# Two expert layers on one core: the shared expert's matrix sums through DRAM, and the sums of x in three steps

## The chip, the cores and the metric

The kernel runs on one core of a Trainium2 chip. The metric is device time in microseconds of one execution; the lower the better. The time before is the median of three runs. Durations of single instructions come from one profiled execution of the same kernel.

The engines go by short names: PE (TensorE, matrix products; PEld is its loading of weights), DVE (VectorE), ACT (ScalarE), POOL (GpSimd), SP (SyncE, which here only issues DMAs). Each takes its instructions strictly in the order of the program.

## The reference

The input x has 16 batches of 256 rows by 256 columns in float32, and cond_8 has 16 rows of 8 logits. Two layers of experts follow, each added to its input:

```
# layer 0: one expert per batch, by the largest logit
expert = argmax(cond_8)
up   = x @ W_up[expert].T   + b_up[expert]
gate = x @ W_gate[expert].T + b_gate[expert]
x = x + (silu(up) * gate) @ W_down[expert].T + b_down[expert]
# layer 1: two experts per batch, weighted, and one shared expert
mlp(x, g, u, d) = (gelu(x @ g) * (x @ u)) @ d
w, sel = top_k(softmax(cond_8), 2);  w = w / sum(w)
x = x + sum_k w_k * mlp(x, skill[sel_k]) + mlp(x, shared)
```

Layer 0's hidden width is 512, layer 1's is 1024. The shared expert of layer 1 has the same three matrices for all 16 batches.

## The kernel before

**Pairs and seven products.** Two batches that use the same expert are worked on as a pair. A pair's matrix product is cut into blocks of two by two, and instead of eight block products the kernel makes seven, with sums of blocks on both sides (Winograd's form of Strassen's method). `STEPS` lists the seven: each has a PSUM bank (X, Y or Q), a block or sum of the weights (A11, A12, A22, and sums S1, S2, nS3, nS4) and a block or sum of the activations (B11, B21, B22, T2, nT1, nT3, nT4). Which batches form pairs is decided from the logits while the kernel runs.

A pair's up phase is cut into quarters: two for layer 0 (`kp` 2) and four for layer 1 (`kp` 4), each with its own 512 KB of gate and up weights. A quarter is the seven products of `up`, of which the seventh (`up(j, 6)`, of the Q bank) is put two steps into the next quarter. In between ACT copies three partial results from PSUM (`copy`, line 504) and DVE makes four blocks of the result (`combine`, line 508): C11, then C12 of the quarter before, C22, C21. The seventh product adds to the Q bank that C22 of its quarter has read. Then `act` applies the activation function: for layer 1 ACT's gelu (line 552) and a product by DVE (line 553), for layer 0 ACT's silu (559) and DVE's line 560. The down phase (`down`) is again seven products, interleaved with the next units' quarters; its late results are DVE's lines 606 and 610.

**Sums.** Three kinds of sums feed the seven products:

- `sums_q` (per quarter) and `sums_d` (per pair) make the four sums of the weight blocks through `sums_a` (lines 468 to 471) on POOL: four instructions of 128x256 elements for a quarter and four of 128x256 (layer 0) or 128x512 (layer 1) for the down weights.
- `sums_x` (per pair) makes the sums of the activations through `sums_b` (lines 461 to 463) on DVE: one instruction of 128x512 and two of 128x256, in the tile `xt` (layer 1) or `bt` with `dz` (layer 0).
- `act_sums` (per quarter) does the same with `sums_b` on the activation's result, a full quarter after it.

**Order.** The order of work is written out when the program is built. `Line` has a clock that each of a quarter's six first products moves by 2 (`UP`), so a quarter is 12. `later(after, f)` puts an action into a list; `flush` emits the due actions, the earliest first and in order of entry among equals. In a quarter that starts at 0, the earlier quarter's seventh product and C12 come at 4, its activation at 6, and its `act_sums` at 12. A pair's down products come at 18 and then every 3 (layer 0), 6 (layer 1) or 4 (three of the shared pairs) after its last quarter.

`ahead(i)`, at the start of quarter i, loads the weights of quarter i+5 (`load_q`, on SP), makes the sums of quarter i+3 (`sums_q`), loads x for a pair that starts at i+3, and, if a pair starts at i+1, calls `sums_x` for it: all three sums are emitted there, before quarter i's own products. The down weights' sums come in the third quarter of a layer-1 pair, and at the end of a layer-0 pair.

**Buffers.** `RINGS` holds the SBUF rings: 6 buffers of quarter weights (`q`), 5 of their sums (`s`), 2 of the down sums (`ds`), 2 of layer 1's x with its sums (`xt`), 7 of activations (`bt`). PSUM has two banks each of X, Y and Q and one each of A and B for the down products; down products of step Y take a bank from the same two as the up products, in turn.

**Units and branches.** With this data the order is: two single batches of layer 0; two pairs of layer 0; a branch on how many further pairs there are (`arms(0)`); then two pairs of layer 0, and the shared pairs 0 to 4 with three more layer-0 pairs after the first three of them; then twelve pairs of sparse experts; a second branch (`arms(1)`); shared pair 5, single batches, three more sparse pairs, and shared pairs 6 and 7. [...] `follow` then sets the list of quarters for the arm and loads the weights of the first quarter that wasn't yet loaded; with `behind=True` three tiny writes to the buffer by DVE, POOL and ACT come first (lines 390 to 392), so that this load, and all that follows it on SP, waits until those engines are in the arm.

Of the kernel before, what the change touches and what calls it, by code (L numbers as in the profile page):

```python
# [8 lines left out]
F32 = mybir.dt.float32  # L9
I32 = mybir.dt.int32  # L10
AF = mybir.ActivationFunctionType
ALU = mybir.AluOpType
# [5 lines left out]
P = 128  # L18
KD = D // P
KPS = (H0 // P // 2, H1 // P // 2)  # L20
# [9 lines left out]
QW = 2 * 4 * P  # L30
# [21 lines left out]
C11, C21, C12, C22 = range(4)  # L52
# [7 lines left out]
def kernel(  # L60
# [10 lines left out]
    nc = tc.nc  # L71
# [5 lines left out]
    dram = ctx.enter_context(tc.tile_pool(name="dram", bufs=1, space=bass.MemoryType.DRAM))  # L77
    ps = ctx.enter_context(tc.tile_pool(name="ps", bufs=1, space=bass.MemoryType.PSUM))

    x1d = dram.tile([B, P, KD, S], F32, name="x1d")  # L80

# [365 lines left out]
    class Pair(Unit):  # L447
# [1 line left out]
        first, step = 18, None  # L449


        def sums_x(self):
            self.x = {n: self.xt[:, i, :] for n, i in B_AT.items()}
            if not self.layer:
                self.x["T2"] = take("dz", S, of=(self, "T2"))
            self.sums_b(self.xt, self.x["T2"])

        @staticmethod
        def sums_b(t, t2):
            tt = nc.vector.tensor_tensor  # L460
            tt(t[:, 4:6, :], t[:, 0:3:2, :], t[:, 2:4, :], ALU.subtract)  # L461
            tt(t2, t[:, C22, :], t[:, 4, :], ALU.add)  # L462
            tt(t[:, 6, :], t[:, C21, :], t2, ALU.subtract)

        @staticmethod
        def sums_a(a, s):
# [5 lines left out]

        def sums_q(self, j):
            s = take("s", QB, of=(self, j))
            s = s[:, :QW].rearrange("p (m k h) -> p m k h", m=2, k=4)
            q = self.q[j]
            self.sums_a(lambda n: q[:, :, A_AT[n], :], lambda n: s[:, :, S_AT[n], :])
            self.s[j] = s
            if not self.layer:
                b = take("bq", 4)  # L480
                nc.gpsimd.tensor_copy(b, self.bq[j])
                self.bq[j] = b

        def sums_d(self):
            s = take("ds", 4, KPS[1], P)
            s = s[:, :, : self.kp]
            d = self.d
            self.sums_a(lambda n: d[:, A_AT[n]], lambda n: s[:, S_AT[n]])
            self.ds = s

        def load_z(self):

# [69 lines left out]

        def act_sums(self, j):
            t = self.acts[j]
            self.sums_b(t, t[:, 2, :])

        def down(self, k):

# [202 lines left out]
    units = [l0_pairs[: NP1 - 2], [*pairs, *shared[NF : NPR - NB]]]  # L771
    tails = [l0_pairs[NP1 - 2 :], shared[-NB : 1 - NB]]
# [7 lines left out]
    def in_order(units):  # L780

        order = []
        for u in units:
            for j in range(u.kp):
                order.append((u, j))
                for p in among[u][j] if u.width == 2 else ():
                    one = p.func.__self__ if isinstance(p, partial) else p.__self__
                    if isinstance(p, partial):
                        order.append((one, p.args[1]))
                    elif p == one.ups:  # L790
                        order += [(one, i) for i in range(one.kp)]
        return order

    quarters = [(u, j) for u in (l0_first, l0_one) for j in range(u.kp)]
    quarters += in_order(units[0] + tails[0])
    Q_AHEAD, S_AHEAD = 5, 3

    class Line:
# [24 lines left out]
        def ahead(self, i):  # L823

            at = dict(enumerate(quarters))
            if i + Q_AHEAD in at:
                u, j = at[i + Q_AHEAD]
                u.load_q(j)
            if i + S_AHEAD in at:
                u, j = at[i + S_AHEAD]  # L830
                if u.width == 2:
                    when_free("s", lambda u=u, j=j: u.sums_q(j))
                if j == 0:
                    if u.width == 2 and not u.layer:
                        when_free("bt", u.load_x)
                    else:
                        if u.layer:
                            self.send(0)
                        u.load_x()
            if i + 1 in at:  # L840
                u, j = at[i + 1]
                if u.width == 2 and j == 0:
                    u.sums_x()
            if i < 0:
                return
            u, j = at[i]
# [55 lines left out]
    line = Line()  # L902
# [52 lines left out]
            quarters[:] = order  # L955
            yield k

    def follow(common, units):

        quarters[common - 4 :] = in_order(units)  # L960
        u, j = quarters[common]
        u.load_q(j, behind=True)

    run(units[0])
    for k in arms(0):
        common = len(quarters)

        mid = [*tails[0]]
        for i, u in enumerate(shared[:NF]):
            mid.append(u)  # L970
            if i < k:
                mid.append(l0_more[i])
                u.step = 4
        places = [a for u in mid for a in among[u]]
        for a in places:
            a.clear()
        pieces = [p for u in l0_ones[2 * k :] for p in (u.ups, u.downs)]
        for a, p in zip(places[3:], pieces):
            a.append(p)
        follow(common, [*mid, *units[1], *tails[1]])  # L980
        run([*mid, *units[1]])
        while line.routed < len(steps):
            line.route()
        for k in arms(1):
            common = len(quarters)
            left = ones[2 * k :]
            rest = [*tails[1], *left[:-1], *more_pairs[:k], *shared[1 - NB :]]
            turns["xs"], turns["d"] = [0, 1], [*turns["d"], 2]
            for u in rest:
                among[u] = [[] for _ in range(u.kp)]  # L990
            if left:

                host = rest[len(left)]
                for j in range(host.kp):
                    among[host][j].append(partial(left[-1].piece, line, j, among=True))
                left[-1].po_bank, left[0].po_bank = "A", "B"
                shared[-NB].first = 24
            follow(common, rest)
            run(rest)
            line.flush(1 << 30)  # L1000
            line.send()
# [58 lines left out]
```

## Time and profile before

| | us |
|---|---|
| median of 3 runs | 1076.67 |
| lowest and highest | 1074.55 and 1078.24 |
| the profiled execution | 1075.29 |
| its span, from first to last instruction | 1073.6 |

The granted TensorE clock is 0.994 over the span. DMA moved 132.35 MB, of which queue q1 (SP's) had 118.88 MB, at a mean of 123 GB/s.

How to read the views that follow: a row of busy times by stage gives the stretch, its length, then for PE, PEld, DVE, ACT and POOL the busy time and the number of instructions, then the granted clock, DMA's busy share and its rate in GB/s. A row of waits names who waited, for what, the total in us, how often, and the longest. A row of the timeline gives the start and length in us, the engine, the line of the kernel, the operation, the tiles (written<-read), their shapes and the number of instructions merged; in brackets stands how long the engine was idle before and what ended that. A matrix product of the program shows as two records, so `x4` on PE is two products of 128x128 weights with 256 columns.

### The profile page before, as it was taken

The numbers are of one execution on the slowest core, as the hardware profiler recorded it, in microseconds if no ns is written. First come the engines' busy times: TensorE is split into PE (matmuls) and PEld (weight loads), VectorE is DVE, ScalarE is ACT, GpSimd is POOL, SyncE is SP. The second block draws the span as 40 slices with busy tenths as digits, with TensorE's granted clock in tenths as the row PEclk, the third lists the DMA queues.
The fourth block names the chain that finished last, engine by engine and source line by source line (L and its number), as shares of the span: only waits on it lengthen the run. The fifth ranks groups of instructions, "written<-read, shape, count | busy, mean of one in ns | idle before, by whom it ended". The sixth has DMA issues, their size and how long they took to land.

```text
span 1073.6 us, 14292 instructions
## 1 busy us (share of the span) xinstructions
PE 1045.7 (97%) x4750; PEld 902.5 (84%) x4750; DVE 805.2 (75%) x1222; ACT 353.5 (33%) x556; POOL 582.8 (54%) x642
## 2 busy tenths in 40 slices
PE   9989999899999999999999999999999999999997
PEld 6777878787878888888888888888888888888886
DVE  7879988888798777777787777777876336787774
ACT  2323333333423333333333333333333123333331
POOL 2837644464476646664675476557623245675520
PEclk9999999999999999999999999999999999999999
DMA  7625443435352542454355335533534545344212
GB/s 249 206 91 167 159 136 109 147 118 135 121 157 80 137 130 89 115 137 117 83 135 138 92 92 136 137 104 89 139 93 132 170 128 157 89 137 129 71 37 43
DMA packets 53203, 132.35 MB, mean 123 GB/s; under 512 B 4850, under 2 KB 24434, under 8 KB 49906
## 3 DMA queue, kind: packets, MB, share of 16 engines
q1 hardware_dynamic: 40562, 118.88, 33.8%
q0 software_dynamic: 12256, 12.06, 8.9%
q8 instruction: 43, 0.70, 0.3%
q14 instruction: 54, 0.44, 0.1%
q10 hardware_dynamic: 288, 0.26, 0.1%
HBM read 110.21 MB, written 20.97 MB: 122 GB/s over the span
## 4 chain that ended last, share of the span: by engine, by line
PE 78%; DVE 15%; issue 4%; ACT 2%; POOL 1%; DMA 0%; SPq 0%; DVEq 0%; ACTq 0%; POOLq 0%
PE X L523 20%; PE Q L523 14%; PE Y L523 13%; PE A L577 11%; PE B L577 8%; PE Y L577 7%; DVE c L508 5%; DVE bt L461 2%; PE X L670 2%; PE Q L670 1%; DVE bt L553 1%; ACT c L552 1%; DVE bt L462 1%; PE A L700 1%; DVE bt L560 1%
## 5 line engine op out<-in xcount | busy, mean ns | idle before, releaser
L504 ACT ACTIVATE cp<-X 128x512 f32<-128x512 f32 x318 | 188.7, 595 | 522.7 <-PE X L523 522.3
L523 PE MATMUL Q<-xt,s 128*128 128x256 f32 x736 | 190.9, 382 | 11.1 <-DVE c L508 11.1
L523 PE MATMUL Y<-xt,q 128*128 128x256 f32 x736 | 190.4, 381 | 3.0 <-DVE ys L610 1.8
L553 DVE TENSOR_TENSOR bt<-c 128x1024 f32<-128x1024 f32 x92 | 129.0, 1402 | 85.1 <-ACT c L552 85.0
L523 PE MATMUL X<-xt,s 128*128 128x256 f32 x736 | 189.3, 380 | 0.0
L523 PEld LDWEIGHTS Q<-xt,s 128*128 128x128 f32 x736 | 139.5, 191 | 33.2 <-issue 13.4
L508 DVE TENSOR_TENSOR c<-cp,Q 128x512 f32<-128x512 f32 x212 | 143.9, 679 | 30.6 <-ACT cp L504 27.7
L468 POOL TENSOR_TENSOR s<-q 128x256 f32<-128x256 f32 x106 | 98.4, 928 | 119.4 <-DMA q<-wq_dram 60.1
L523 PEld LDWEIGHTS Y<-xt,q 128*128 128x128 f32 x736 | 138.4, 190 | 26.7 <-DVE c L508 4.7
L523 PEld LDWEIGHTS X<-xt,s 128*128 128x128 f32 x736 | 139.3, 190 | 20.8 <-issue 2.1
L471 POOL TENSOR_TENSOR s<-s,q 128x256 f32<-128x256 f32 x106 | 83.5, 788 | 131.5 <-PE Q L523 131.5
L508 DVE TENSOR_TENSOR c<-cp,Y 128x512 f32<-128x512 f32 x212 | 143.8, 678 | 10.0 <-PE Y L523 9.3
L440 POOL DMA_DIRECT2D out_dram<-ys x46 | 49.6, 1079 | 154.1 <-DVE c L508 62.3
L552 ACT ACTIVATE c<-c 128x1024 f32<-128x1024 f32 x92 | 96.8, 1052 | 35.6 <-DVE c L508 35.4
L469 POOL TENSOR_TENSOR s<-s,q 128x256 f32<-128x256 f32 x106 | 101.8, 961 | 9.3 <-PE A L700 1.1
L461 DVE TENSOR_TENSOR bt<-bt 128x512 f32<-128x512 f32 x113 | 105.4, 933 | 0.9 <-DMA bt<-x_dram 0.8
L577 PE MATMUL B<-bt,ds 128*128 128x256 f32 x424 | 102.3, 382 | 0.0
L577 PE MATMUL A<-bt,ds 128*128 128x256 f32 x424 | 101.5, 379 | 0.0
L470 POOL TENSOR_TENSOR s<-q 128x256 f32<-128x256 f32 x106 | 98.7, 931 | 0.0
L523 PE MATMUL X<-xt,q 128*128 128x256 f32 x368 | 94.4, 379 | 0.0
L577 PEld LDWEIGHTS B<-bt,ds 128*128 128x128 f32 x424 | 81.1, 191 | 11.5 <-ACT ys L715 0.3
L577 PEld LDWEIGHTS A<-bt,ds 128*128 128x128 f32 x424 | 80.4, 190 | 11.4 <-POOL s L469 0.3
(163 smaller groups left out, 1239.1 us busy)
## 6 DMA issues: line engine op xcount, KB each, us to landing
q<-wq_dram SPq DMA_DIRECT2D x100, 512.0 KB, 3.6
d<-wd_dram SPq DMA_DIRECT2D x22, 1024.0 KB, 6.2
xt<-x1d SPq DMA_DIRECT2D x46, 256.0 KB, 4.5
out_dram<-ys POOLq DMA_DIRECT2D x46, 256.0 KB, 4.5
q<-wq_dram SPq DMA_DIRECT2D x16, 514.0 KB, 3.6
d<-wd_dram SPq DMA_DIRECT2D x7, 513.0 KB, 4.5
bt<-x_dram SPq DMA_DIRECT2D x14, 256.0 KB, 4.9
x1d<-ys SPq DMA_DIRECT2D x14, 256.0 KB, 3.4
```

Of the source, the lines that this page charges most:

```text
L440: nc.gpsimd.dma_start(row(out), ys[:, :, t, :], accum_op=ALU.add)
L461: tt(t[:, 4:6, :], t[:, 0:3:2, :], t[:, 2:4, :], ALU.subtract)
L468: tt(s("S1"), a("A21"), a("A22"), ALU.add)
L469: tt(s("S2"), s("S1"), a("A11"), ALU.subtract)
L470: tt(s("nS3"), a("A21"), a("A11"), ALU.subtract)
L471: tt(s("nS4"), s("S2"), a("A12"), ALU.subtract)
L504: nc.scalar.activation(t, self.banks["X", j], AF.Copy)
L508: nc.vector.tensor_tensor(self.c[j][:, block].rearrange("p m s -> p (m s)"), self.copies[n, j], self.banks[tag, j], op,)
L523: nc.tensor.matmul(self.banks[tag, j][:, bass.ts(m, S)], lhsT=self.q[j][:, m, A_AT[a], :] if a in A_AT else self.s[j][:, m, S_AT[a], :], r ...
L552: nc.scalar.activation(u, u, AF.Gelu_apprx_tanh)
L553: nc.vector.tensor_tensor(t[:, 0:4, :], u, v, ALU.mult)
L577: nc.tensor.matmul(d, lhsT=src[:, j, :], rhs=self.acts[j][:, B_AT[b], :], start=OPENS[k] and j == 0, stop=j == self.kp - 1, skip_group_che ...
```

## The change

There are three edits.

1. **Sums of the shared expert's matrices.** Two kinds of DRAM tiles are added, `qsums` (four of 128x1024 elements) and `dsums` (128x2048). The first shared pair makes its sums as before, on POOL, and stores each to DRAM by a DMA that POOL issues. The seven other shared pairs make no sums; SP loads them from DRAM into the same ring buffers, at the same points of the order.
2. **Sums of x.** `sums_b` returns three actions instead of emitting three instructions. When the quarter before a pair belongs to a pair as well, `sums_x` enters them at 2, 6 and 10 of that quarter's clock instead of emitting them all at its start. `act_sums` emits its three as before.
3. **The branches.** `follow` now finds the place of the first new quarter from the line's position, and the three tiny writes are left out at layer 0's branch. They stay at layer 1's.

```diff
+    qsums = [dram.tile([P, QW], F32, name=f"qsums{j}") for j in range(KPS[1])]
+    dsums = dram.tile([P, 4 * KPS[1] * P], F32, name="dsums")
...
-        def sums_x(self):
+        def sums_x(self, spread):
+
             self.x = {n: self.xt[:, i, :] for n, i in B_AT.items()}
             if not self.layer:
                 self.x["T2"] = take("dz", S, of=(self, "T2"))
-            self.sums_b(self.xt, self.x["T2"])
+            for i, f in enumerate(self.sums_b(self.xt, self.x["T2"])):
+                if spread:
+                    line.later(2 + 4 * i, f)
+                else:
+                    f()
...
         def sums_b(t, t2):
             tt = nc.vector.tensor_tensor
-            tt(t[:, 4:6, :], t[:, 0:3:2, :], t[:, 2:4, :], ALU.subtract)
-            tt(t2, t[:, C22, :], t[:, 4, :], ALU.add)
-            tt(t[:, 6, :], t[:, C21, :], t2, ALU.subtract)
+            return (
+                lambda: tt(t[:, 4:6, :], t[:, 0:3:2, :], t[:, 2:4, :], ALU.subtract),
+                lambda: tt(t2, t[:, C22, :], t[:, 4, :], ALU.add),
+                lambda: tt(t[:, 6, :], t[:, C21, :], t2, ALU.subtract),
+            )
...
         def sums_q(self, j):
             s = take("s", QB, of=(self, j))
-            s = s[:, :QW].rearrange("p (m k h) -> p m k h", m=2, k=4)
+            flat = s[:, :QW]
+            s = flat.rearrange("p (m k h) -> p m k h", m=2, k=4)
+            self.s[j] = s
+            if self.at is None and self is not shared[0]:
+                nc.sync.dma_start(flat, qsums[j])
+                return
             q = self.q[j]
             self.sums_a(lambda n: q[:, :, A_AT[n], :], lambda n: s[:, :, S_AT[n], :])
-            self.s[j] = s
+            if self is shared[0]:
+                nc.gpsimd.dma_start(qsums[j], flat)
...
         def sums_d(self):
             s = take("ds", 4, KPS[1], P)
-            s = s[:, :, : self.kp]
-            d = self.d
+            self.ds = s[:, :, : self.kp]
+            flat = s.rearrange("p k j h -> p (k j h)")
+            if self.at is None and self is not shared[0]:
+                nc.sync.dma_start(flat, dsums)
+                return
+            d, s = self.d, self.ds
             self.sums_a(lambda n: d[:, A_AT[n]], lambda n: s[:, S_AT[n]])
-            self.ds = s
+            if self is shared[0]:
+                nc.gpsimd.dma_start(dsums, flat)
...
-                    u.sums_x()
+                    u.sums_x(i > 1 and at[i][0].width == 2)
...
-    def follow(common, units):
-
-        quarters[common - 4 :] = in_order(units)
-        u, j = quarters[common]
-        u.load_q(j, behind=True)
+    def follow(units, behind=True):
+
+        known, start = len(quarters), line.at + 1
+        quarters[start:] = in_order(units)
+        if known == start + Q_AHEAD - 1:
+            u, j = quarters[known]
+            u.load_q(j, behind=behind)
...
-        follow(common, [*mid, *units[1], *tails[1]])
+        follow([*mid, *units[1], *tails[1]], behind=False)
...
-            follow(common, rest)
+            follow(rest)
```

More of the change, by code (lines that the diff above doesn't have):

```diff
@@ L564, in act_sums @@
             t = self.acts[j]
-            self.sums_b(t, t[:, 2, :])
+            for f in self.sums_b(t, t[:, 2, :]):
+                f()
         def down(self, k):
@@ L956, in arms @@
             yield k
-    def follow(common, units):
-        quarters[common - 4 :] = in_order(units)
-        u, j = quarters[common]
-        u.load_q(j, behind=True)
+    def follow(units, behind=True):
[4 more added lines that the diff above has]
+            u.load_q(j, behind=behind)
     run(units[0])
     for k in arms(0):
-        common = len(quarters)
-        mid = [*tails[0]]
+        mid, further = [*tails[0]], l0_more[:k]
         for i, u in enumerate(shared[:NF]):
             mid.append(u)
-            if i < k:
-                mid.append(l0_more[i])
+            if i < len(further):
+                mid.append(further[i])
                 u.step = 4
@@ L984 @@
         for k in arms(1):
-            common = len(quarters)
             left = ones[2 * k :]
```

## The prediction

> **What bounds the kernel now.** I read the busy times first, then PE's waits and the busy times by stage, then the timeline around each wait.
>
> ```profile
> PE 1045.7 (97%) x4750; PEld 902.5 (84%) x4750; DVE 805.2 (75%) x1222; ACT 353.5 (33%) x556; POOL 582.8 (54%) x642
> ...
> 64.00:340.00 276.00, 263.65 (x1178) 225.05 (x1177) 234.08 (x359) 95.37 (x147) 153.34 (x168) 0.98 0.44 136
> 340.00:790.00 450.00, 449.50 (x2077) 393.83 (x2077) 344.45 (x484) 157.71 (x248) 274.78 (x269) 1.00 0.42 113
> ...
> PE Q L523 <- DVE c L508: 9.6, 5, 2.5
> PE Y L523 <- DVE ys L610: 1.8, 2, 1.6
> PE Y L523 <- DVE c L508: 0.8, 2, 0.5
> ```
>
> PE is the bound. The two stage rows give length, then PE, PEld, DVE, ACT and POOL. Four matmul records follow at 0.86 us, 0.216 us each. In 340 to 790 us 2,077 of them need 448.6 of 450.0 us: at most 1.4 us can be won there. In the stage where layer 0's pairs and the shared expert's first five pairs alternate (68 to 336.5 us), 1,154 records need 249.3 of 268.5 us: 19.2 us are lost. The last three rows, of 64 to 340 us, say to what: combinations of products that DVE delivers late. By the timeline the 19.2 us are 1.9 at 104 us; 2.5, 5.1, 4.4 and 3.4 where four shared pairs pass to the next pair (142, 200, 259, 318 us); and 1.9 in small waits. This is such a passing:
>
> ```profile
> 193.14 1.21 DVE L461 TENSOR_TENSOR bt<-bt 128x512 f32<-128x512 f32 x1
> 193.76 1.17 POOL L471 TENSOR_TENSOR s<-s,q 128x256 f32<-128x256 f32 x1
> 194.38 0.83 DVE L462 TENSOR_TENSOR dz<-bt 128x256 f32<-128x256 f32 x1
> 195.25 0.83 DVE L463 TENSOR_TENSOR bt<-bt,dz 128x256 f32<-128x256 f32 x1
> ...
> 197.31 1.06 ACT L552 ACTIVATE c<-c 128x1024 f32<-128x1024 f32 x1 [3.82 <-DVE c L508]
> ...
> 198.40 1.23 DVE L553 TENSOR_TENSOR bt<-c 128x1024 f32<-128x1024 f32 x1 [1.12 <-ACT c L552]
> 199.54 0.68 DVE L508 TENSOR_TENSOR c<-cp,Q 128x512 f32<-128x512 f32 x1
> ...
> 200.37 1.36 PE L523 MATMUL Q<-xt,s 128*128 128x256 f32 x4 [2.51 <-DVE c L508]
> 201.53 1.91 PE L523 MATMUL X<-dz,s 128*128 128x256 f32 x4
> ```
>
> The three sums of x stand in one burst before combinations C11 and C12 (196.01, 196.60), so ACT's function, its product (L553) and C22 (199.54) come late, and PE's seventh product waits 2.51 us. Then eight matmuls run at 0.427 us: another 1.7 us.
>
> The other stage where sums of x occur, at a passing with no wait:
>
> ```profile
> 745.23 0.68 DVE L461 TENSOR_TENSOR xt<-xt 128x512 f32<-128x512 f32 x1
> 745.95 0.42 DVE L462 TENSOR_TENSOR xt<-xt 128x256 f32<-128x256 f32 x1
> 746.41 0.43 DVE L463 TENSOR_TENSOR xt<-xt 128x256 f32<-128x256 f32 x1
> ...
> 751.17 1.71 DVE L553 TENSOR_TENSOR bt<-c 128x1024 f32<-128x1024 f32 x1 [0.83 <-ACT c L552]
> 751.76 1.71 POOL L470 TENSOR_TENSOR s<-q 128x256 f32<-128x256 f32 x1
> 752.80 0.68 DVE L508 TENSOR_TENSOR c<-cp,Q 128x512 f32<-128x512 f32 x1
> 753.39 0.67 DVE L508 TENSOR_TENSOR c<-cp,Y 128x512 f32<-128x512 f32 x1
> ...
> 754.33 1.03 PE L523 MATMUL Y<-xt,q 128*128 128x256 f32 x4
> ```
>
> Here the burst lies in DVE's idle time. L553 waits for ACT, which PE paces. C21 (753.39) ends at 754.06, and the next pair's Y product, which takes the bank that C21 reads because a down product took the other, starts at 754.33. A DVE end reaches PE 0.06 us later, so C21 has 0.21 us to spare.
>
> **What the Trainium skill says.** "SBUF — State Buffer", Who interferes with whom: a DVE instruction with two SBUF inputs and a GpSimd instruction that reads SBUF exclude each other for a whole instruction. The trace agrees: L470 (0.73 alone) lasts 1.71 and ends 0.59 after L553; L461 takes 0.68 alone and 1.21 beside POOL, L462 and L463 0.42 and 0.83. "TensorE: Matmul & The Clock Gate", What's actually happening: after an idle window of some 3.4 us the clock is halved. Here waits of 2.5 us were enough, and one of 1.76 was not. "Runtime: NRT & Kernel Launch", Instruction fetch mechanics: a taken branch can wait for a fetch. The trace has PE idle for 3.42 us at layer 0's branch, with nothing else awaited.
>
> **The sums kept in DRAM.** Of eight shared pairs, seven lose 4 x 4 POOL instructions of 128x256 and 4 of 128x512, and gain 4 loads of 512 KB and one of 1 MB on SP. In the mixed stage that is 16 sets of about 3.5 us and four of 6.2: some 80 of POOL's 153 us. POOL isn't waited for by PE here; the gain is DVE's end of lock waits. The loads are issued three quarters (at least 18 us) ahead; a 1 MB load lands in 6.2 us. They stand in SP's queue behind the q load, whose buffer is released later than theirs, so they block nothing; a d or x load behind them comes some 3 us later, with more spare than that. The added 21 MB over the whole run meet DMA engines that are 44% busy: nothing, at worst 2 us. The first pair's five stores cost POOL about 1.08 each (the row of out_dram<-ys), 5.4 us near 104 us, where POOL is also making its sums: 0 to 1 us, taken within the 104 us term.
>
> **The spread, at the mixed passings.** Worked for the one at 200. At 180.15 an L461 took 1.54 beside POOL's sums of d: 0.86 less, and DVE runs without a pause from there, so the activation's sums start at 189.90 instead of 190.74. With start-to-start times of DVE without POOL (0.72, 0.46, 0.46; first sum of x 0.72; C11 0.60), C12 starts at 192.86 and ends at 193.54. ACT then takes to 194.63, L553 to 195.88, the second sum 0.46, and C22 ends at 196.96. The seventh product is due at 197.17: no wait. One quarter on the same chain (third sum, C21, sums, C11, C12, ACT, L553) ends C22 at 203.83, due 203.2: 0.75 of wait and 0.1 of restart. So 5.1 becomes 0.9: 4.2 saved. The third passing likewise saves 3.5, the fourth 2.5, the first 1.3, since POOL still makes that pair's sums. At 104 us the burst moves but the lock stays: 1.0 (0 to 1.9). A wait near 335 us, behind POOL's sums of d, goes: 0.7. Sum 13.2; low end 9 (104 unchanged, some 0.8 left more at each passing), high end 17 (nearly all of 19.2). At 57.5 us a wait of 0.4 goes too.
>
> **The spread, at the passings between sparse pairs.** The second sum comes due together with L553 and was entered later, so it stands behind L553; the third stands between C22 and C21. Neither has cover: 0.46 each. And POOL's L470, locked out by L553, goes first (to 753.47), so the second sum ends near 753.75 and costs 0.91. C21 is 1.37 later, less 0.21 to spare: PE waits 1.16, plus 0.1 of restart, 1.26. L553 is 1.70 to 1.73 at ten passings from 423 to 751 us and at 940.7: 11 x 1.26 = 13.9. Where L553 is 1.23 (787.8 and 1013.8) or gets to be so (977, whose POOL sums go), 0.33 each, 1.0; two near 350 and 387 have 0.86 to spare: 0.3. Sum 15.2. If the lock cost nothing, 11 x 0.82 and the rest: 10. If the two early ones fall into the locked pattern: 17.5.
>
> **The rest.** DVE reaches layer 1's branch later by about 0.5, which lengthens the wait of 1.54 at 801 by that. Near 84 us a ys is 0.2 late. The touch: three tiny instructions (0.06, 0.09, 0.20) go, and SP, which stood from 45 to 67 us, loads two q 9 to 17 us sooner. POOL's 10.8 us wait for q at 71 goes, but its next instruction still waits for a d load at 87, and PE waited for neither. PE's fetch of 3.42 us and the slow clock behind it (1.7) stay. A q load then falls beside the fetch: -1 to +1, taken as 0. A touched or untouched fetch that hits would give 5.
>
> **Sum.** -13.2 - 0.4 + 15.2 + 0.5 + 0.2 = +2.3 on the profiled execution's 1075.29 (span 1073.6): 1077.6. The median of the runs is 1.4 above that execution, so 1079.
>
> **Rivals.** (A) Slower: DVE stays the bound in the mixed stage. It was busy 234 of 276 us there and the new sums stand before C22, so seventh products still wait. For it: the waits are of one in-order chain with ACT's 1.06 in it. Against: half of POOL's locks go. It decides where C22 stays over 1.5 us late; then only about 5 of the 13.2 come and the time is 1087. (B) Faster: the cost at the sparse passings isn't there, because the late sums fall into idle time of DVE or the Y bank isn't the one C21 holds. For it: PE waits nowhere at these places today. Against: C22 starts as L553 ends (752.88) and C21 0.59 later, at full rate, with no idle time between. Without most of it, 1079 - 13 = 1066. (C) The loads or the fetch collide with other DMA and add several us: 1090; against it, 44% load.
>
> **Chances.** Forecast (1075 to 1084) 0.50, A 0.20, B 0.25, C 0.05. About 0.3%, or 3.2 us, is what a measurement can tell from no change. B and a little of the forecast are faster: 0.25. The forecast straddles the bound: 0.30 within, the rest slower: 0.45. The forecast's own bounds (gains 9 to 17, losses 10 to 17.5) give 1070 to 1086; the range takes in most of A and B: 1068 to 1088.
>
> **What would show it.** Right: waits of Y for c L508 of about 1 us at some eleven passings after 415 us, PE below 440 of the 450 us of 340 to 790; L508's waits of Q in the mixed stage below 1 us, clock back to 1.00 but for the branch; POOL busy near 440 us. Wrong: no Y waits (B), or Q waits above 1.5 us left (A), or waits for s that name a DMA (C).

## The result, and the profile after

Changed kernel: 1071.98 us, median of five runs (1070.21 to 1073.54). Kernel before: 1076.67 (1074.55 to 1078.24). The ratio is 0.9961, with a 95% interval from 0.9942 to 0.9979: faster by 0.4%, where the forecast was 1079. The profiled execution took 1071.98 (span 1070.3, granted clock 0.997), against 1075.29 (span 1073.6, 0.994) before. The forecast had added 1.4 us to the profiled execution for the median; this time the two are the same.

The page of the changed kernel, its busy times and, at the end, its DMA issues (KB each, then median us to landing):

```profile
PE 1043.4 (97%) x4750; PEld 899.6 (84%) x4750; DVE 784.6 (73%) x1221; ACT 353.2 (33%) x555; POOL 449.7 (42%) x506
...
s<-qsums SPq DMA_DIRECT2D x28, 512.0 KB, 4.7
...
ds<-dsums SPq DMA_DIRECT2D x7, 1024.0 KB, 6.1
```

POOL is down from 582.8 to 449.7 us, near the forecast's 440, and the 28 + 7 loads land in 4.7 and 6.1 us (medians). DVE executes almost the same instructions as before in 20.6 us less: that is, on balance, lock time that has gone.

The same two stages by windows of the changed kernel (length, then PE, PEld, DVE, ACT, POOL, granted clock, DMA share, GB/s):

```profile
64.00:340.00 276.00, 272.54 (x1244) 235.75 (x1243) 228.82 (x379) 100.50 (x155) 84.39 (x97) 0.99 0.59 193
340.00:790.00 450.00, 441.20 (x2021) 381.59 (x2020) 343.56 (x471) 152.74 (x241) 254.84 (x247) 1.00 0.42 114
```

In the mixed stage PE fits 1,244 matmul records into the 276 us, where before it had 1,178; in the sparse stage it had time for 2,021 where it had 2,077. One stage won, the other lost. PE's waits in the changed kernel, first of the whole execution, then of 340 to 790 us (us in total, times, longest):

```profile
PE Y L544 <- DVE c L529: 8.9, 15, 0.8
PE Q L544 <- DVE c L529: 2.9, 3, 1.8
PE X L544 <- issue: 2.8, 1, 2.8
PE Y L544 <- DVE ys L632: 2.2, 1, 2.2
```

```profile
PE Y L544 <- DVE c L529: 8.4, 13, 0.8
```

The lines have moved: L470 to L472 are the old L461 to L463 (sums of activations), L480 the old L470 (POOL), L529 the old L508 (combinations), L544 the old L523 (products), L573 and L574 the old L552 and L553 (activation), L632 the old L610. The Y waits that the prediction asked for are there, nine of 0.83 us and some short ones; PE is busy for 441.2 of the 450 us, just above the 440 that it asked for. The Q waits of the mixed stage are gone but for one of 0.7 us. No row names a DMA as what `s` was waited for.

Both traces hold 4,750 matmul records in the same order, so they can be paired one to one; the shift is how much later a matmul starts after than before. Its steps say where the time went:

| stretch (us of before) | forecast | measured | difference |
|---|---|---|---|
| start to 68: layer 0's branch | -0.4 | -2.5 | -2.1 |
| 68 to 110: the wait at 104 | -0.8 | +2.0 | +2.8 |
| 110 to 340: mixed passings | -12.2 | -14.9 | -2.7 |
| 340 to 790: sparse passings | +13.3 | +12.7 | -0.6 |
| 790 to the end | +2.4 | -0.6 | -3.0 |
| whole span | +2.3 | -3.4 | -5.7 |

The forecast column is the prediction's sum, sorted by place: of the 15.2 us at the sparse passings, one of the eleven dear ones (940.7) and two of the cheap ones lie behind 790 us, 1.9 together.

This is the mixed passing that was shown of before, now by the timeline of the changed kernel:

```profile
187.41 0.69 DVE L470 TENSOR_TENSOR bt<-bt 128x512 f32<-128x512 f32 x1
188.01 0.68 DVE L529 TENSOR_TENSOR c<-cp,Y 128x512 f32<-128x512 f32 x1
188.60 0.68 DVE L529 TENSOR_TENSOR c<-cp,Q 128x512 f32<-128x512 f32 x1
...
190.51 1.23 DVE L574 TENSOR_TENSOR bt<-c 128x1024 f32<-128x1024 f32 x1 [1.22 <-ACT c L573]
191.65 0.42 DVE L471 TENSOR_TENSOR dz<-bt 128x256 f32<-128x256 f32 x1
191.98 0.68 DVE L529 TENSOR_TENSOR c<-cp,Q 128x512 f32<-128x512 f32 x1
...
193.14 1.03 PE L544 MATMUL Q<-xt,s 128*128 128x256 f32 x4
```

The first sum takes 0.69 us where it took 1.21. C22 (191.98) ends at 192.66, and the seventh product (193.14) waits for nothing.

And a sparse passing of the same kernel:

```profile
710.30 0.73 POOL L479 TENSOR_TENSOR s<-s,q 128x256 f32<-128x256 f32 x1
...
710.40 1.71 DVE L574 TENSOR_TENSOR bt<-c 128x1024 f32<-128x1024 f32 x1 [0.82 <-ACT c L573]
710.98 1.71 POOL L480 TENSOR_TENSOR s<-q 128x256 f32<-128x256 f32 x1
712.03 0.94 DVE L471 TENSOR_TENSOR xt<-xt 128x256 f32<-128x256 f32 x1
712.89 0.68 DVE L529 TENSOR_TENSOR c<-cp,Q 128x512 f32<-128x512 f32 x1
713.49 0.41 DVE L472 TENSOR_TENSOR xt<-xt 128x256 f32<-128x256 f32 x1
713.83 0.68 DVE L529 TENSOR_TENSOR c<-cp,Y 128x512 f32<-128x512 f32 x1
714.56 1.13 PE L544 MATMUL Y<-xt,q 128*128 128x256 f32 x4 [0.83 <-DVE c L529]
```

Read it from the top. POOL's L479, which started 0.10 us earlier, holds up L574 (1.71 us, where it takes 1.23 alone), and L574 holds up POOL's L480, so L480 ends at 712.69. The second sum, next in DVE's queue, cannot run beside it and takes 0.94 instead of 0.42. The third (0.41) stands between the two combinations. C21 ends at 714.51, and PE starts 0.05 later, having waited 0.83.

### The profile page after: what moved, and what is told of

Its sections match the earlier page's. It is cut to its first block, busy times and chain, and to the rows that moved or that the text cites. A ratio compares the mean times of both kernels' runs of the same rounds, so it can differ in the third digit from the quotient of the medians.

```text
span 1070.3 us, 14116 instructions
## 1 busy us (share of the span) xinstructions
PE 1043.4 (97%) x4750; PEld 899.6 (84%) x4750; DVE 784.6 (73%) x1221; ACT 353.2 (33%) x555; POOL 449.7 (42%) x506
## 4 chain that ended last, share of the span: by engine, by line
PE 80%; DVE 12%; ACT 3%; issue 3%; POOL 0%; DMA 0%; SPq 0%; DVEq 0%; ACTq 0%; POOLq 0%
PE X L544 20%; PE Q L544 14%; PE Y L544 14%; PE A L599 11%; PE B L599 8%; PE Y L599 5%; DVE c L529 5%; DVE bt L574 3%; ACT c L573 2%; PE X L692 2%; PE Q L692 2%; DVE bt L470 1%; DVE xt L471 1%; PE A L722 1%; ACT dz L621 1%
## 5 line engine op out<-in xcount | busy, mean ns | idle before, releaser
L544 PE MATMUL Y<-xt,q 128*128 128x256 f32 x736 | 192.7, 384 | 11.5 <-DVE c L529 8.9
L574 DVE TENSOR_TENSOR bt<-c 128x1024 f32<-128x1024 f32 x92 | 128.7, 1399 | 94.4 <-ACT c L573 94.4
L544 PE MATMUL Q<-xt,s 128*128 128x256 f32 x736 | 189.6, 380 | 2.5 <-DVE c L529 2.5
L544 PE MATMUL X<-xt,s 128*128 128x256 f32 x736 | 189.5, 380 | 0.0
L544 PEld LDWEIGHTS Y<-xt,q 128*128 128x128 f32 x736 | 137.9, 191 | 39.8 <-DVE c L529 19.4
L529 DVE TENSOR_TENSOR c<-cp,Q 128x512 f32<-128x512 f32 x212 | 144.2, 680 | 32.4 <-ACT cp L525 28.2
L544 PEld LDWEIGHTS Q<-xt,s 128*128 128x128 f32 x736 | 139.3, 190 | 23.6 <-DVE c L529 4.9
L544 PEld LDWEIGHTS X<-xt,s 128*128 128x128 f32 x736 | 139.3, 190 | 20.5 <-ACT cp L525 1.4
L529 DVE TENSOR_TENSOR c<-cp,Y 128x512 f32<-128x512 f32 x212 | 144.0, 679 | 15.2 <-PE Y L544 10.2
L478 POOL TENSOR_TENSOR s<-q 128x256 f32<-128x256 f32 x78 | 70.2, 900 | 125.0 <-PE Q L544 61.9
L481 POOL TENSOR_TENSOR s<-s,q 128x256 f32<-128x256 f32 x78 | 63.6, 815 | 106.1 <-PE Q L544 102.8
L573 ACT ACTIVATE c<-c 128x1024 f32<-128x1024 f32 x92 | 96.8, 1052 | 20.8 <-DVE c L529 20.8
L470 DVE TENSOR_TENSOR bt<-bt 128x512 f32<-128x512 f32 x113 | 101.3, 897 | 0.3 <-DMA bt<-x_dram 0.2
L544 PE MATMUL X<-xt,q 128*128 128x256 f32 x368 | 94.4, 379 | 0.0
L599 PE MATMUL Y<-bt,d 128*128 128x256 f32 x376 | 90.0, 379 | 0.0
L479 POOL TENSOR_TENSOR s<-s,q 128x256 f32<-128x256 f32 x78 | 78.0, 1000 | 7.1 <-PE A L722 1.1
```

The lines of the kernel that those rows point to most:

```text
L470: lambda: tt(t[:, 4:6, :], t[:, 0:3:2, :], t[:, 2:4, :], ALU.subtract),
L478: tt(s("S1"), a("A21"), a("A22"), ALU.add)
L479: tt(s("S2"), s("S1"), a("A11"), ALU.subtract)
L481: tt(s("nS4"), s("S2"), a("A12"), ALU.subtract)
L529: nc.vector.tensor_tensor(self.c[j][:, block].rearrange("p m s -> p (m s)"), self.copies[n, j], self.banks[tag, j], op,)
L544: nc.tensor.matmul(self.banks[tag, j][:, bass.ts(m, S)], lhsT=self.q[j][:, m, A_AT[a], :] if a in A_AT else self.s[j][:, m, S_AT[a], :], r ...
```

## The experiments

All were run with the kernel before on the same chip; a ratio is to that kernel, with its 95% interval. "Shift" is the same pairing with before, one profiled execution each. The edits are to the changed kernel unless another is named. "Burst" means that the three sums of x stand together, as before.

| kernel | median us (range) | ratio | to 68 | 68-110 | 110-340 | 340-790 | 790-end |
|---|---|---|---|---|---|---|---|
| e1 DRAM sums alone | 1058.28 (1056.60-1061.79) | 0.9848 [0.9824, 0.9872] | -2.6 | +0.9 | -14.1 | +0.4 | -1.9 |
| e2 spread alone | 1085.46 (1084.73-1086.45) | 1.0093 [1.0071, 1.0115] | -0.9 | -0.9 | -2.4 | +12.6 | +2.8 |
| e3 touch left out alone | 1076.83 (1074.25-1080.13) | 1.0017 [1.0007, 1.0028] | -1.8 | -0.5 | +0.6 | +0.3 | +0.3 |
| e4 spread at mixed only | 1058.79 (1056.69-1062.42) | 0.9851 [0.9826, 0.9876] | -2.8 | -1.2 | -13.8 | +1.5 | -0.8 |
| e5 e1 + writes by POOL | 1061.14 (1060.29-1062.33) | 0.9860 [0.9843, 0.9876] | -0.2 | -0.1 | -14.8 | +1.1 | -0.8 |
| e6 e1 + sums by POOL | 1077.66 (1073.85-1081.55) | 1.0014 [1.0000, 1.0028] | -1.0 | -0.1 | +2.0 | +0.5 | -0.9 |
| e7 second sum early | 1063.04 (1062.27-1063.05) | 0.9872 [0.9856, 0.9889] | -0.1 | -0.4 | -14.0 | +3.2 | -1.0 |
| e8 all before L574 | 1061.35 (1059.68-1061.53) | 0.9854 [0.9837, 0.9870] | +1.5 | -0.7 | -14.4 | +0.9 | -1.1 |
| e9 no spread | 1061.04 (1057.80-1061.82) | 0.9863 [0.9844, 0.9882] | -2.5 | +0.2 | -14.0 | 0.0 | -1.2 |
| e10 quarters' sums alone | 1062.24 (1060.70-1065.01) | 0.9867 [0.9844, 0.9890] | -1.6 | +2.6 | -9.4 | -0.4 | -1.5 |
| e11 down sums alone | 1064.39 (1062.77-1065.47) | 0.9887 [0.9866, 0.9907] | -0.7 | 0.0 | -7.0 | +0.3 | -2.5 |

### The three parts, each alone

e1, the sums in DRAM with burst and touch:

```
-u.sums_x(i > 1 and at[i][0].width == 2)
+u.sums_x(False)
...
-follow([*mid, *units[1], *tails[1]], behind=False)
+follow([*mid, *units[1], *tails[1]])
```

> Only the sums through DRAM; the sums of x in one burst and the touch as before. Theory (the locks): nearly all of the 14.7 us gained at the mixed passings comes from POOL's missing sums. At the passing at 200 us the burst puts C22 0.46 us later than with the spread, so Q waits of about 0.4 there and about 13 us gained in all, no waits at the sparse passings, 3.4 us of fetch and its slow clock at layer 0's branch: about 1063 to 1065. Rival (the spread): the order of the sums made the gain; then Q waits of 1.5 us or more stay at four passings and the time is 1070 to 1075.

e2, the spread with touch and with POOL's sums:

```
-if self.at is None and self is not shared[0]:
-    nc.sync.dma_start(flat, qsums[j])
-    return
...
-if self is shared[0]:
-    nc.gpsimd.dma_start(qsums[j], flat)
...
-follow([*mid, *units[1], *tails[1]], behind=False)
+follow([*mid, *units[1], *tails[1]])
```

and the same for `dsums`.

> Only the spread; POOL makes all sums and the touch stays. Theory (the locks): the four mixed passings keep Q waits of 1 to 2 us (3 to 5 us gained in all), the sparse passings cost 1.1 us each at eleven places, those near 751 and 941 us included because POOL has sums there again, 1 to 2 us lost near 104 us: about +9 to +12, 1086 to 1088. Rival (the spread): the mixed passings are healed without DRAM, about -12 there, and the time is 1075 to 1078.

e3 has neither spread nor DRAM sums; only the touch is left out, as in the changed kernel.

> Only the touch behind layer 0's branch left out. Theory (the touch): it is what made PE's wait at that branch shorter (2.8 for 3.4 us) and kept the clock: about -2.4, 1074.3. Rival (chance of place): the fetch takes the same and the slow clock after it depends on where the wait falls; then the time is within 1 us of before and the eight slow matmuls behind the branch are there in some runs and not in others, or stay.

Against 1075.02 us on that chip, the DRAM sums alone bring 16.7, the spread alone costs 10.4, and leaving out the touch costs 1.8 (0.8 to 3.0 by the interval). Together they make -4.5; the changed kernel stands at -4.7. The change is a large gain and a large loss, and each is worth nearly as much with the other as without it.

The surprise is at the mixed passings. The prediction worked both parts there in one sum, under the spread's name. By the table e1, with its burst, gains 14.1 us there, and the changed kernel 14.9. The passing of e1, by its timeline:

```profile
187.45 0.68 DVE L470 TENSOR_TENSOR bt<-bt 128x512 f32<-128x512 f32 x1
188.16 0.42 DVE L471 TENSOR_TENSOR dz<-bt 128x256 f32<-128x256 f32 x1
188.62 0.42 DVE L472 TENSOR_TENSOR bt<-bt,dz 128x256 f32<-128x256 f32 x1
188.97 0.68 DVE L529 TENSOR_TENSOR c<-cp,Y 128x512 f32<-128x512 f32 x1
...
192.51 0.68 DVE L529 TENSOR_TENSOR c<-cp,Q 128x512 f32<-128x512 f32 x1
```

The three sums are done in 1.59 us (187.45 to 189.04), against 2.94 before (193.14 to 196.08), C22 ends at 193.19, and PE starts its seventh product at 193.24. The burst was never too long; it was locked. Alone the spread wins only 2.4 us in this stretch, and the waits stay, by the waits of e2 from 64 to 340 us:

```profile
PE Q L534 <- DVE c L519: 7.1, 5, 1.9
```

e9 confirms it from the other side: the changed kernel with `u.sums_x(False)`, so that DRAM sums and the missing touch are left.

> Sums through DRAM and the touch left out, no spread: the changed kernel less its second edit. Theory: the touch is worth nothing either way (PE's fetch of 3.5 to 4 us is the same, the slow clock behind it comes and goes with where the wait falls): within 2 us of the sums through DRAM alone, 1057 to 1060. Rival: without the spread the loads started early collide with the fetch or with POOL's first sums, and it is 1062 or more.

It gains 14.0 us in the stretch and loses nothing from 340 to 790 us. The changed kernel is e9 with the spread. Each against the kernel before on its own chip, e9 gains 14.8 us and the changed kernel 4.7; in the mixed stage the spread saves 0.9.

### Where the spread costs

e4 keeps the spread at the mixed passings and takes it away where the next pair is sparse:

```
-u.sums_x(i > 1 and at[i][0].width == 2)
+u.sums_x(i > 1 and at[i][0].width == 2 and u not in units[1] + more_pairs)
```

> The changed kernel, with the sums of x in one burst again where the pair to come is of sparse experts. Theory: the 12.8 us lost between 338 and 777 us come from the second and third sum behind L574 (the activation's product); without them the Y waits of 0.83 there are gone and the mixed stage is as in the changed kernel: 1060 to 1063. Rival: the loss there comes from something else that the change brought (SP's or DMA's new loads, POOL's new timing); then little of it comes back, 1069 to 1072.

At 1058.79 it is as fast as e1. From 340 to 790 us it loses 1.5 us where the changed kernel loses 12.7. So the loss belongs to the spread at sparse passings.

Two kernels then ask what in it costs: that there are three places, or that one of the places stands behind L574. e7 brings the second sum to the first's place and leaves the third where it was:

```
-line.later(2 + 4 * i, f)
+line.later((2, 2, 10)[i], f)
```

> The changed kernel with the first two sums of x entered at 2 and the third at 10. Theory (lock and order): only the third sum (0.46) stands between L574 and C21 then, no sum meets POOL's locked-out instruction, and Y waits of about 0.25 us, 0.35 with the restart, stay at the nine sparse passings that now lose 1.1 each: about -6.8, 1065. Rival (order alone, no lock): the second sum cost the same as the third, 0.46 each, so 4 us come back: 1068.

e8 has three places too, all ahead of L574:

```
-line.later(2 + 4 * i, f)
+line.later((2, 4, 5)[i], f)
```

> The changed kernel with the three sums of x at 2, 4 and 5: spread, but all entered ahead of the activation that comes at 6. Theory: what cost 12.8 us is the place behind L574, not the spreading; before it DVE waits for ACT, so the sums are free there, the sparse passings have no wait above 0.1 us, and the time is that of the burst with DRAM, 1057 to 1060. Rival: any spreading delays C21 or C12 and some of the loss stays, 1063 or more.

e7 loses 3.2 us from 340 to 790, e8 0.9. A sparse passing of e7, by its timeline:

```profile
666.45 1.71 DVE L574 TENSOR_TENSOR bt<-c 128x1024 f32<-128x1024 f32 x1 [0.82 <-ACT c L573]
667.04 1.71 POOL L480 TENSOR_TENSOR s<-q 128x256 f32<-128x256 f32 x1
668.08 0.67 DVE L529 TENSOR_TENSOR c<-cp,Q 128x512 f32<-128x512 f32 x1
668.68 0.41 DVE L472 TENSOR_TENSOR xt<-xt 128x256 f32<-128x256 f32 x1
669.01 0.67 DVE L529 TENSOR_TENSOR c<-cp,Y 128x512 f32<-128x512 f32 x1
669.74 1.13 PE L544 MATMUL Y<-xt,q 128*128 128x256 f32 x4
```

L574 is locked as before, but what follows it is C22, which reads PSUM and starts at once beside POOL's L480. The third sum alone moves C21 by 0.33, little more than the spare time. PE starts 0.23 to 0.25 us later at each of the nine passings, where the changed kernel loses 1.1; the median, 1063.04, lies below both figures that were expected. So it is the second sum, an instruction with two SBUF inputs right behind a lock, that doubles and carries the loss.

### What the DRAM sums win: locks, not work

Two kernels on e1 put POOL's time back. In both the loads stay and overwrite what POOL wrote. e5 lets POOL only write, eight memsets ahead of each load:

```
+for n in (*range(4), *range(4)):
+    nc.gpsimd.memset(s[:, :, n, :], 0.0)
 nc.sync.dma_start(flat, qsums[j])
...
+for n in (*range(4), *range(4)):
+    nc.gpsimd.memset(s[:, n], 0.0)
 nc.sync.dma_start(flat, dsums)
```

> The kernel with the sums through DRAM alone, and POOL writes zeros into each buffer (eight instructions that read nothing, of the sums' size) before the load overwrites them, so POOL stays busy at the old places. Theory (the lock): DVE was slowed by POOL instructions that read SBUF beside its own with two SBUF inputs; writes alone don't hold it, the bt sums keep 0.68 and 0.42 us at the mixed passings, and the time is 1057 to 1061. Rival (POOL's work): it was POOL being busy, or POOL's place in the order; then the long forms of 1.2 and 0.83 us come back beside the memsets and the time is 1067 or more.

e6 lets POOL make the sums as before:

```
+self.sums_a(lambda n: q[:, :, A_AT[n], :], lambda n: s[:, :, S_AT[n], :])
 nc.sync.dma_start(flat, qsums[j])
...
+self.sums_a(lambda n: d[:, A_AT[n]], lambda n: s[:, S_AT[n]])
 nc.sync.dma_start(flat, dsums)
```

> The same, but POOL makes the sums as before and the load overwrites them with the stored ones: the loads are there, the reads too. Theory (the lock): all of the gain is gone and the time is that of before, 1074 to 1077; the loads themselves cost under 1 us. Rival: the loads or the new waits bring a gain or a loss of their own, and the time is off by more than 3 us.

e5 keeps the gain, e6 loses all of it. The groups of POOL in e5 from 64 to 340 us (out, shape, count, busy us, mean ns of one, then idle before them):

```profile
L490 POOL MEMSET s<- 128x256 f32 x128 | 35.5, 413 | 39.5 <-PE Q L548 36.8 <-PE X L548 2.7
L508 POOL MEMSET ds<- 128x512 f32 x32 | 15.3, 523 | 0.5 <-PE B L603 0.5
```

In these 276 us POOL is busy for 135.93 in e5, 88.63 in e1 and 153.34 in before, and DVE does not notice. The first sums of x and of the activations on DVE, one row of its groups from 105 to 336 us, in e5 and then in e6:

```profile
L470 DVE TENSOR_TENSOR bt<-bt 128x512 f32<-128x512 f32 x29 | 21.1, 729 | 0.0
```

```profile
L470 DVE TENSOR_TENSOR bt<-bt 128x512 f32<-128x512 f32 x27 | 25.1, 931 | 0.0
```

729 ns with POOL writing, 931 with POOL reading (908 in the kernel before), and 743 in e1, where POOL does neither. The means include sums that meet those that POOL still makes for other pairs. In the whole trace of e5, five sums of 128x512 and 32 of 128x256 have memsets and nothing else of POOL beside them; they take 683 and 425 ns, the same as the 73 and 159 with no POOL instruction beside them. PE's waits of e6 from 64 to 340 us are those of before:

```profile
PE Q L548 <- DVE c L533: 9.9, 4, 2.8
```

So the loads cost little or nothing (e6, which has them on top of all that before does, stands at 1.0014 of it), and POOL's being busy cost little either: e5 is 2.9 us above e1, on another chip (0.9860 of the kernel before against 0.9848), and its trace puts 2.4 of that ahead of 68 us, at the branch. What cost was POOL's reading of SBUF beside DVE. The Trainium skill, "SBUF — State Buffer", Who interferes with whom, makes the same distinction; e5 and e6 are this case's proof of it.

Which of the sums held the locks? e10 and e11 are e1 with only the quarters' sums, or only the sums of d, through DRAM. e10:

```
-if self.at is None and self is not shared[0]:
-    nc.sync.dma_start(flat, dsums)
-    return
...
-if self is shared[0]:
-    nc.gpsimd.dma_start(dsums, flat)
```

and e11 the same for `qsums`.

> Only the quarters' sums go through DRAM; POOL makes the down weights' sums of all pairs (7 x 6.2 us of reading POOL instructions stay, 28 x 3.5 us go). Theory: the sums that are locked out beside the passings are mostly the quarters', so most of the gain stays: 1060 to 1064. Rival: the sums of the down weights, which lie at the third quarter just ahead of a passing, start the delay: 1066 to 1070.

> Only the down weights' sums go through DRAM; POOL makes the quarters' sums of all pairs. Theory: little is gained, since C12, the activation and C22 at the passings still wait for sums beside POOL: Q waits of 1 to 2 us stay, 1069 to 1073. Rival: 1062 to 1066.

e10 wins 13.6 us and e11 11.5, by the medians, against 1075.85 on their chip; together 25, where both at once win 16.7. In the mixed stage of the profiled executions the parts are 9.4 and 7.0, against 14.1, and PE's waits of Q there are 1.8 and 4.9 us, where before had 9.6. For e11 the rival's figure was the nearer one: the theory had put nearly all the gain on the quarters' sums. A likely reason for the overlap is that both relieve the same chain of DVE, and that a wait ends as soon as C22 is in time; no run shows it, and part of the 25 may be scatter, since the profiled executions of the two, the slowest of four each, have spans only 10.3 and 9.9 us shorter than before.

### Layer 0's branch

The prediction left the wait at the branch and the slow clock behind it as they were. In the changed kernel they became 2.81 us and nothing:

```profile
62.27 1.10 PE L544 MATMUL X<-bt,q 128*128 128x256 f32 x4 [2.81 <-issue]
...
64.07 1.03 PE L599 MATMUL B<-bt,ds 128*128 128x256 f32 x4
```

In e8, which has the same branch and no touch either, the wait is 3.81 us, and the half clock is there. Four matmuls need 1.03 us at full clock and 1.91 at half. Over all kernels the half clock goes neither with the touch nor with the length of the wait. It was there in before (3.42), e2 (2.61), e5 (3.38), e6 (3.01), e7 (3.72), e8 (3.81), e10 (3.07) and e11 (3.16); it was not there in the changed kernel (2.81), e1 (3.08), e3 (3.58), e9 (2.81) and e4 (0.70). The stretch up to 68 us swings between +1.5 and -2.8 us on this account. Since the touch, the DRAM sums and the spread each occur on both sides, none of them decides it, and I don't count the 2.1 us as something that the change does. In e4 PE came to the branch some 2 us later, after half clock from 52 us on, and waited only 0.70: PE's branch instruction takes 3.2 to 4.3 us in every kernel, beginning at 57.6 to 58.9 us, while matmuls are still in the queue, so lateness before it is absorbed.

The clock records of the traces show what decides it. In before the half clock is granted from 64.54, 201.08 and 259.10 us, each time for 3.413 us (in e8 once for 6.827, two steps). The distances, 136.53 and 58.03 us, are 40 and 17 times 3.413: the clock is set on a grid of steps of that length. Its place in the span differs between executions (the border after 60 us lies at 61.13 in before, 60.86 in the changed kernel, 62.73 in e2, 61.16 in e3). These are the steps around the wait, first of e2, then of e3:

```profile
59.32:62.73 3.41, 0.80 (x5) 0.51 (x4) 3.41 (x8) 0.20 (x1) 0.93 (x2) 1.00 0.01 2
62.73:66.14 3.41, 3.41 (x10) 2.66 (x9) 1.51 (x4) 0.60 (x1) 0.00 (x0) 0.50 0.03 7
```

```profile
57.75:61.16 3.41, 1.67 (x7) 0.87 (x5) 2.96 (x5) 1.81 (x3) 3.41 (x5) 1.00 0.47 133
61.16:64.57 3.41, 1.57 (x7) 1.44 (x8) 3.19 (x7) 0.43 (x1) 1.72 (x3) 1.00 0.11 35
64.57:67.98 3.41, 3.41 (x17) 3.00 (x16) 0.45 (x1) 0.49 (x2) 0.73 (x1) 1.00 0.01 2
```

The shorter wait of e2 lies inside one step, in which PE was busy for 0.80 us, and the next step has the half clock. The longer one of e3 is cut by a border into steps with 1.67 and 1.57 us, and the clock stays whole. In all 13 traces, by the profile's busy times, a half step behind a step of full clock always follows one in which PE was busy for at most 0.45 of it, and never one with 0.46 or more; between 0.42 and 0.45 both outcomes occur. So at this branch the half clock depends on where the wait falls on the grid, and as far as this change is concerned that is chance.

e3's median is 1.8 us above that of before, while its profiled execution, the fastest of its 22, has a span 1.0 us shorter. The mean granted clock of these 22 executions is 0.9935, of the 27 of before 0.9955. An estimate from that is 0.0020 x 1075 = 2.1 us, so more half clock can account for the 1.8; at which waits no trace here shows.

The fastest version found is e1, at 0.9848 of before, with e4 beside it (1058.79); their ranges overlap almost whole. Both beat the changed kernel by some 12 us, by their ratios.

## Why the prediction was wrong

The forecast was +2.3 us on the span and came to -3.4. Two sums, some -13 and +15, nearly cancelled in it, so errors of two or three microseconds decided the sign. Two steps failed. The waits that the forecast left at the mixed passings mostly didn't come (the stretch is 2.7 us below the forecast), and neither did the locks that it kept at passings behind 790 us (3.0 us below). The other three differences, -2.1, +2.8 and -0.6, cancel by luck. The terms in turn:

**The sparse passings, "The spread, at the passings between sparse pairs": right in mechanism; the total up to 790 us agrees partly by luck.** 12.7 us against 13.3. The instruction named (the second sum behind POOL's L480, at 0.91) was measured at 0.94, and the wait at 0.83, some 1.1 with its restart, against 1.16 and 1.26. Rival B, that this cost isn't there, fell: nine such passings from 413 to 714 us. They make 9.9 us, where the forecast had ten at 1.26, 12.6. The two early passings cost 0.44 each, 0.9 for 0.3. Most of the remaining 1.9 us comes from short waits in the middle of pairs, which the forecast didn't have. Such waits come and go, between -0.4 and +0.5 us each, in the kernels without the spread too.

**The passings at 751 us and behind 790 us: a step that failed.** At 751 and 940.7 us I took the lock from the trace of before and kept it. But POOL runs some five quarters ahead, and the sums that stood beside those two passings were the shared expert's own, which the first part of the change takes away. In e2, where POOL makes them, the two passings do cost 1.1 us each. In the changed kernel L574 is unlocked there; this is the first of the two:

```profile
748.05 1.23 DVE L574 TENSOR_TENSOR bt<-c 128x1024 f32<-128x1024 f32 x1 [0.83 <-ACT c L573]
749.19 0.42 DVE L471 TENSOR_TENSOR xt<-xt 128x256 f32<-128x256 f32 x1
...
750.46 0.68 DVE L529 TENSOR_TENSOR c<-cp,Y 128x512 f32<-128x512 f32 x1
751.21 1.11 PE L544 MATMUL Y<-xt,q 128*128 128x256 f32 x4
```

Two places at 1.26 and three at 0.33 became about 0.1 each; three of the five (940.7, 977 and 1013.8) lie behind 790, and 1.9 us of forecast became 0.3. With the 0.5 forecast at layer 1's branch, of which 0.2 came, and a tail 0.6 us shorter, this makes most of the 3.0 us. The prediction had unlocked the passing at 977 for this reason, and not asked it of 751 and 940.7.

**The mixed passings, "The spread, at the mixed passings": the other step that failed, in size, and the part credited to the spread isn't there.** The section's durations were those without POOL, so the locks' gain was in its sum; but it moved the sums as well, and did not ask what the old burst would give. e1 and e9 have all but 0.8 and 0.9 us of the gain without it; e2, with the spread and without the DRAM sums, has 2.4 of it. By passing, the gains were 2.4, 4.9, 4.3 and 2.3 us, where the forecast had 1.3, 4.2, 3.5 and 2.5. The first was forecast low because POOL still makes that pair's sums; nearly all of its 2.5 us came back all the same. At the other three the forecast left "0.75 of wait and 0.1 of restart" one quarter on. At the fourth this wait came (0.73 at 310 us); at the second and third it did not. Of the rest, small waits before 136 us gave 0.9 that wasn't forecast, and the wait near 335 us gave 0.2 instead of 0.7. The 0.9 before 136 us is all that the spread adds in this stage: e1 and e9 lose some 0.15 there, and at the passings they gain as much as the changed kernel.

These rows, at the second passing, of the changed kernel follow those of its mixed passing above:

```profile
198.58 0.68 DVE L529 TENSOR_TENSOR c<-cp,Q 128x512 f32<-128x512 f32 x1
...
199.40 1.07 PE L544 MATMUL Q<-bt,s 128*128 128x256 f32 x4
```

At the passing shown C22 had 0.48 us to spare, not 0.21; the next C22 came 6.60 us after it (198.58 - 191.98), not 6.87; and the product that waits for it was due 6.26 us after the seventh (199.40 - 193.14), not 6.03. Three terms of a quarter of a microsecond each, all read slightly against the change, turned 0.14 us of spare time into 0.63 of lateness: some 0.8 us that didn't come, there and at the third passing. Rival A (C22 still late) took the same chain further in the wrong direction.

**The wait at 104 us: wrong in sign in this execution, and the cause stays open.** I forecast -1.0, since the burst moves. By the timeline of the changed kernel:

```profile
99.99 0.94 DVE L471 TENSOR_TENSOR xt<-xt 128x256 f32<-128x256 f32 x1
100.86 0.68 DVE L529 TENSOR_TENSOR c<-cp,Q 128x512 f32<-128x512 f32 x1
101.45 0.41 DVE L632 TENSOR_TENSOR ys<-dz,Y 128x256 f32<-128x256 f32 x1
...
101.92 2.08 PE L544 MATMUL Y<-xt,q 128*128 128x256 f32 x4 [2.25 <-DVE ys L632]
```

POOL still makes its sums here, so the second sum, now behind L581 (layer 0's product with the bias), is locked at 0.94 as at a sparse passing, and stands ahead of the L632 that PE's Y bank waits for. The wait went from 1.62 to 2.25, and the matmuls behind it run at half clock, which is another 1.6. The sum can't be the whole reason: e2 and e4 have it at the same place and as long (0.94 at 100.40 and 98.25 us), and PE waits only 1.07 and 0.77 there, at full clock; e10, with the burst, waits 1.88 and has the half clock. So half of the forecast's gain came in e2, none here, and what sets the length of this wait no run shows.

**Layer 0's branch, "PE's fetch of 3.42 us and the slow clock behind it (1.7) stay".** In this execution they did not: 2.1 us. The experiments show that this comes and goes in kernels with and without the touch, with the wait's place on the clock's grid. The prediction's reading that waits of 2.5 us were enough to halve the clock was too simple: in the same trace a wait of 2.46, at 318 us, left it whole. The Trainium skill, "Runtime: NRT & Kernel Launch", Instruction fetch mechanics, has the branch waiting for a fetch; that agrees with the 3.2 to 4.3 us, and the touch didn't change it.

**The parts priced at nothing** were so within what can be told: the loads (e6, 0 to 3 us by its interval), their place in SP's queue (PE waits for no load of `s`, `ds`, `q` or `d`), the 10.8 us of POOL's wait. Rival C fell.

## What to carry to other kernels

When two engines share a port, count which instructions *read* at the same time, not how busy the engines are: here POOL's summing of the same matrices again cost PE some 16 us through the DVE instructions that its reads stretched, and 86 us of pure writes in their place (POOL busy 535.0 us in e5, 448.5 in e1) took back 2.9 at most. Before spreading a burst over a queue, look at what each new place stands behind: an instruction with two SBUF inputs directly behind one that has locked POOL out pays double, one that stands behind a PSUM read doesn't. And where a change has two parts, price the second on the machine that the first leaves, since a lock or a wait in the old trace may belong to work that is gone.

## What the runs showed of the hardware

- POOL instructions that only write SBUF left DVE's two-input instructions at full rate: in e5, 683 ns for 128x512 and 425 for 128x256 beside memsets alone, as beside nothing; in e6, with POOL's sums in that place, the mean for 128x512 was 931.
- When POOL has been locked out by a long DVE instruction and DVE's next instruction also has two SBUF inputs, POOL goes first: L480 ended at 712.69 and the 128x256 sum started at 712.03 ended 0.28 us after it, at 712.97. All nine such passings show the same 0.28. If DVE's next reads PSUM, both run at once (C22, 668.08, 0.67).
- Waits of 2.6 to 3.8 us at one and the same branch left the clock halved in eight kernels and whole in four others, with no order by length: behind a wait of 3.58 it was whole, behind one of 2.61 it was half.
- The half clock came in whole steps of 3.413 us, on a grid that lies differently in each execution. It followed steps of full clock with PE busy for at most 45% of the 3.413 us, and never one with 46% or more, in the 13 traces.
